# A graph network on one core: 24 instead of 20 of 98 receiver blocks fetched edge by edge, their products placed by time

## The chip, the cores and the metric

The kernel runs on one core of one Trainium2 chip. The metric is device time in microseconds (us) of one execution. The kernel before has a median of 2966.63 us over 10 runs (2956.32 to 2979.18). TensorE multiplies, VectorE (DVE), ScalarE (ACT) and GpSimd (POOL) do the elementwise work, SyncE (SP) issues transfers; POOL also issues the indirect transfers, whose row numbers come from a list on the chip.

## The reference

There are 12500 nodes with 64 features, and 212500 edges sorted by receiver (100000 drawn pairs in both directions and a loop on each node). Cut to what is computed:

```python
def sage(h, Wl, Wr, b):                    # three of these; relu after the first two
    summed = segment_sum(h[src], dst, n)
    cnt = segment_sum(ones(n_edges), dst, n)
    return (summed / maximum(cnt, 1))[...] @ Wl + h @ Wr + b

h = relu(layernorm(x))
x = x + sage(relu(sage(relu(sage(h, ...)), ...)), ...)
h = relu(layernorm(x))
agg = scatter_mean(edge_attr_64, dst)      # of the edges' 64 features
y = relu(concat([agg, h]) @ W0 + b0)
y = relu(y @ W1 + b1) @ W2 + b2
return x + y
```

All is fp32. The kernel splits an fp32 value into three bf16 terms of 64 columns each (192 columns a node), so that sums of them keep the precision.

## The kernel before

**Tiling.** The receivers are 98 blocks of 128 nodes (`NB = 98`). The sum over the neighbours of a block is made in one of two ways. *Fetched* blocks are the first `GB = 20`: a block has at most `EK = 19` times 128 edges; for each 128 edges POOL gathers the senders' rows from DRAM (`got`, 128 x 192 bf16, L461), DVE makes the one-hot matrix of their receivers (`own`, L336, for five products at a time), and TensorE adds their product into `pg` (L489, 128x192). *Dense* blocks are the other 78, in groups of four (`dense_groups`: 19 full groups and one of two blocks): there is a matrix of edge counts from all 12544 senders to the group's 512 receivers, stored as one byte per count and read as fp8. A group takes 98 *whole* products (L392, 128 rows of senders by 512 receivers, the first two bf16 terms, 128 columns of the array) and 98 *half* products (L403, the third term, 64 columns of the array, by turns in its left and right half).

**Stages.** Layer 0 builds the matrices as well: a pair of one-hot tiles (`h` and `c`, DVE, L790 to L792) is multiplied into `pb` (L809, 104 products per group), ACT casts it into the matrix (`m`, L812), and SP stores the matrix (`mat`, L834). Layer 1 reads the matrices back (`t`, L1005). Layer 2 does that too, and also sums the edge features (L1138, 19 products for each of all 98 blocks, with `load` and `cut` ahead of them) and runs the last network on each group (L1167, L1177, L1186).

**The order.** TensorE's order is written out by `Weave`. `run` yields the whole products of a group to position 56 (`TURN`), as many half products, then the remaining 42 of both. Other work is put between them: `wide` work when the count of whole products `w` passes its position, `narrow` work at a given index of a half phase. `spread` puts the use of each fetched product into `wide`, at equal distances (`spot`), so fetched products stand among whole products alone. Their use number i issues the fetch of number i + `NGOT`, as the buffer comes free. `pg` is a tile of two halves, allocated anew for every two blocks, in a pool of one buffer; after each block DVE reduces its half into `ga` (L496), and after every four come transposes (L507), the blocks' own rows turned (L425) and the mixing with the weights (L436 and L440). In layer 0 the matrix fills are spread over 40 `wide` places and, two at a time, over the half-phase indices 6, 20, 34, 48, 62 and 76.

**Index and lists.** In layer 0 `index` finds where each group's edges begin: ACT counts in `heads`, POOL gathers a tile of receivers (`ends`, L567 through `gather`, two buffers), ACT counts in it (L582), and POOL gathers the edges (`to`, `of`). `coded` does that for dense groups, `listed` for four fetched blocks; the latter also has POOL gather the block's 19 x 128 receivers and senders (`l_to`, `l_of`: eight gathers for four blocks), from which DVE makes `place` and `rows_of` (L748 to L756). These steps are hung at fixed distances before the first use of their blocks, or before the start of their group.

Of the kernel before, what the change touches and what calls it, by code (L numbers as in the profile page):

```python
# [11 lines left out]
F32 = mybir.dt.float32  # L12
I32 = mybir.dt.int32
# [6 lines left out]
ALU = mybir.AluOpType  # L20
# [9 lines left out]
P = 128  # L30
D = 64
# [12 lines left out]
WD = 5  # L44
FAR = 1 << 23
EK = 19
GB = 20
H1 = 10
QE = 5

# [21 lines left out]
def in_order(  # L72
# [217 lines left out]
    assert HP % HC == 0  # L290
    RING = HP // HC
    TURN = 2 * HC * (-(-RING // 2))

    class Weave:

        def __init__(self):
            self.w, self.seq, self.wides, self.narrows = 0, 0, [], []

        def wide(self, pos, fn):
            self.seq += 1
            heapq.heappush(self.wides, (pos, self.seq, fn))

        def narrow(self, pos, sub, fn):
            self.seq += 1
# [2 lines left out]
        def run(self, whole, half):  # L309


            half = enumerate(half)
            for n in (TURN, None):
                for _ in islice(whole, n):
                    self.w += 1
                    while self.wides and self.wides[0][0] <= self.w:
                        heapq.heappop(self.wides)[2]()
                for i, _ in islice(half, n):
                    due = [f for f in self.narrows if f[0] <= i and f[1] <= self.w]
                    for f in sorted(due):  # L320
                        self.narrows.remove(f)
                        f[3]()
                    heapq.heapify(self.narrows)

        def rest(self):
            while self.wides or self.narrows:
# [17 lines left out]
    HALVES = ((0, H1), (H1, EK))  # L344
    CUTS = [(k, min(k + QE, EK)) for k in range(0, EK, QE)]
    NC = len(CUTS)
    NGOT = 8

    psd = ctx.enter_context(tc.tile_pool(name="ps_dense", bufs=1, space=PSUM))
    psc = ctx.enter_context(tc.tile_pool(name="ps_conv", bufs=1, space=PSUM))  # L350
    psg = ctx.enter_context(tc.tile_pool(name="ps_got", bufs=1, space=PSUM))
    conv = ctx.enter_context(tc.tile_pool(name="conv", bufs=2))
    gots = ctx.enter_context(tc.tile_pool(name="got", bufs=NGOT))
    owns = ctx.enter_context(tc.tile_pool(name="own", bufs=2))

    class Layer:


        def __init__(self, l, rows, done, gap=0, kept=(conv, 2)):
            self.l, self.rows, self.done, self.gap, self.kept = l, rows, done, gap, kept  # L360
            self.psd, self.psc, self.psg = psd, psc, psg
            self.pool, self.got, self.own = conv, gots, owns
            self.weave = Weave()
            self.turns = 0
            self.fetched, self.owned = {}, {}

# [8 lines left out]
        def hand_over(self, to):  # L375

            w = self.weave
            for pos, _, f in sorted(w.wides, key=lambda a: a[:2]):
# [100 lines left out]
        def use(self, i):  # L479
            b, k = divmod(i, EK)  # L480
            if i == 0:
                self.mark(0, 0)
            if i % (2 * EK) == 0:
                self.pg = self.psg.tile([P, 2, 3 * D], F32, name="pg")
            if i % (4 * EK) == 0:
                self.ga = self.pool.tile([P, 4, D], F32, name="ga", bufs=2)
            if k % QE == 0:
                self.mark(b, k // QE + 1)
            nc.tensor.matmul(  # L489
                self.pg[:, b % 2, :], self.owned.pop(i), self.fetched.pop(i),  # L490
                start=k == 0, stop=k == EK - 1,
            )
            self.fetch(i + NGOT)
            if k + 1 < EK:
                return
            nc.vector.tensor_reduce(  # L496
                self.ga[:, b % 4, :],
                self.pg[:, b % 2, :].rearrange("p (i d) -> p d i", i=3), axis=AX.X, op=ALU.add,
            )
            if b % 4 == 3:  # L500
                ga, j0, w = self.ga, b - 3, self.weave
                box = {}

                def sums():
                    pt = self.psc.tile([D, 4, P], F32, name="pt")
                    for k in range(4):
                        nc.tensor.transpose(pt[:, k, :], ga[:, k, :], ident)  # L507
                    box["agg"] = self.pool.tile([D, 4 * P], F32, name="gat", bufs=1)
                    nc.scalar.copy(box["agg"], pt.rearrange("p k n -> p (k n)"))

                def own_rows():
                    ht = self.turn(j0, 4)
                    w.wide(w.w + 9, lambda: self.mix(box["agg"], ht, j0, 4, inv_u))

                w.narrow(w.w + 1, 40, sums)
                w.narrow(w.w + 1, 68, own_rows)

    steps = NB * len(dense_groups)

    def spot(i, first):  # L520
# [2 lines left out]

    def spread(layer, first):
        for i in range(EK * GB):
            layer.weave.wide(spot(i, first), lambda i=i: layer.use(i))


    TW = 4 * P
# [14 lines left out]
    with ExitStack() as s:  # L544
# [8 lines left out]
            steps = relu_steps(layer.pool, o, t)  # L553
            return steps + [lambda: nc.sync.dma_start(h_d[1][:, j0 : j0 + n, :], t)]

        layer = Layer(0, rows0, done0, gap=6)
        heads = s.enter_context(tc.tile_pool(name="heads", bufs=1)).tile([P, TT], I16, name="heads")
        out0 = s.enter_context(tc.tile_pool(name="out0", bufs=2))
        idx = s.enter_context(tc.tile_pool(name="idx", bufs=1))
# [12 lines left out]
        def index(j, box):  # L572
# [17 lines left out]
            def ends():  # L590

                box["tile"] = tile("tile_of", 1)
                nc.vector.tensor_scalar(
                    box["tile"], box["s"], -0.5, 1.0 - TT / 2, op0=ALU.mult, op1=ALU.max
                )
                tile_i = tile("tile_i", 1, I32)
                nc.vector.tensor_scalar(tile_i, box["tile"], TT / 2 - 1.0, None, op0=ALU.add)
                box["ends"] = tile("ends", TW, I32)
                gather(box["ends"], tiles_d, tile_i[:, :1])

            def inside():
# [321 lines left out]
        with tc.manual_schedule(engines={PE, DVE, ACT, POOL}):  # L923
# [96 lines left out]
    def load(b):  # L1020
        if b is None:
            return

        n = EK * P
        raw = ed.tile([P, n // P * D + 1], F32, name="raw")
        first = raw[:1, n // P * D :].bitcast(I32)
        nc.vector.tensor_scalar(first, mine[:1, b : b + 1], float(EP - n), None, op0=ALU.min)
        at0 = nc.values_load(
            first, engines=[SP], min_val=0, max_val=EP - n,
            skip_runtime_bounds_check_because="it is clamped, and is not under 0",  # L1030
        )
        raw = raw[:, : n // P * D].rearrange("p (k d) -> p k d", d=D)
        nc.sync.dma_start(raw, edge[ds(at0, n), :].rearrange("(p k) d -> p k d", k=EK))
# [4 lines left out]
        nc.sync.dma_start(to, dst[ds(at0, n), :].rearrange("(p k) o -> p (k o)", k=EK))  # L1038
# [739 lines left out]
```

## Time and profile before

| What | Value |
|---|---|
| median of 10 runs | 2966.63 us |
| the profiled execution | 2959.17 us, of which the span is 2957.3 us |
| mean granted TensorE clock | 0.983 |
| layer 0, 1, 2 (from first whole product to the next layer's) | 94 to 1166, 1166 to 1938, 1938 to 2957 us |
| TensorE, whole products (L392) | 5880, 378 ns from start to end, overlapping |
| TensorE, half products (L403) | 5880, 375 to 381 ns, overlapping |
| TensorE, fetched products (L489) | 1140, 247 ns |
| POOL, fetches (L461) | 1140, 1094 ns mean, 1247.4 us in all |
| DMA | 537.43 MB, mean 182 GB/s |
| SP, stores of matrices | 39 of 3136 KB |

The profile is of one execution. Busy time of an engine counts its instructions' spans; matmuls overlap, so what one costs is read from the distance of starts. "Idle before" a group of instructions is the time in which its engine stood, with what ended it. The chain of waits goes back from the last instruction to what released it, step by step. A stretch (window) gives each engine's busy time within it, and the granted clock.

### The profile page before, as it was taken

The page shows a single profiled execution, that of the slowest core. Times are in us where ns is not written, and L with a number is a line of the kernel's source. Part 1 is how long each engine was busy: PE and PEld are TensorE (multiplying, and loading weights), DVE is VectorE, ACT ScalarE, POOL GpSimd, SP SyncE. Part 2 cuts the span into 40 slices and gives each one's busy share as a digit, 9 for nine tenths or more (in the row PEclk, how much of TensorE's full clock was granted, in tenths as well). Part 3 has the DMA queues.
Part 4 walks back from the last instruction along what each step waited for, and adds up shares of the span by engine and source line. Part 5 has one row for each costly group of instructions (what it writes and reads, how often), then busy time and mean ns, then how long its engine had stood idle before and what let it go on. Part 6 is the DMA issues. An engine that isn't in the chain of part 4 may idle for free.

```text
span 2957.3 us, 50078 instructions
## 1 busy us (share of the span) xinstructions
PE 2767.3 (94%) x19505; PEld 1603.0 (54%) x19505; DVE 1630.7 (55%) x3376; ACT 1122.4 (38%) x2339; POOL 1428.5 (48%) x1313
## 2 busy tenths in 40 slices
PE   1699998999999998999999999999999999999997
PEld 0455554555555554555555555565656656565655
DVE  8878777787777772211111111156756656566663
ACT  4666565566666562100000000033333333333332
POOL 5346666566565550455545454434544444445440
PEclk9999999999999999999999999999999999999997
DMA  3434443434434435765645665576767576676661
GB/s 95 173 111 169 159 148 140 161 130 161 164 126 162 164 135 206 230 210 204 208 162 204 207 208 182 182 256 221 223 210 231 175 223 221 213 223 223 209 205 35
DMA packets 203193, 537.43 MB, mean 182 GB/s; under 512 B 83873, under 2 KB 92194, under 8 KB 197954
## 3 DMA queue, kind: packets, MB, share of 16 engines
q1 hardware_dynamic: 143890, 458.08, 42.7%
q0 software_dynamic: 41360, 66.33, 9.7%
q10 hardware_dynamic: 17696, 9.74, 1.1%
q8 instruction: 154, 2.52, 0.4%
q14 instruction: 93, 0.76, 0.1%
HBM read 391.11 MB, written 142.90 MB: 181 GB/s over the span
## 4 chain that ended last, share of the span: by engine, by line
PE 83%; DVE 10%; issue 2%; DMA 1%; ACT 1%; POOL 1%; another core or an unknown queue 0%; SPq 0%; ACTq 0%; DVEq 0%; POOLq 0%
PE p L392 38%; PE p L403 21%; PE pb L809 6%; PE pe L1138 5%; PE pg L489 3%; DVE c L792 3%; PE po L436 3%; PE po L440 3%; PE pt L425 2%; DVE h L790 1%; PE pm L1177 1%; DVE h L791 1%; PE pm L1186 1%; DMA ends<-in_dst_dram,tile_i 1%; PE pm L1167 0%
## 5 line engine op out<-in xcount | busy, mean ns | idle before, releaser
L461 POOL DMA_INDIRECT got<-h_d,rows_of x1140 | 1247.4, 1094 | 1307.6 <-PE pg L489 864.5
L812 ACT CAST m<-pb 128x490 uint16<-128x490 f32 (+1 forms) x1014 | 545.6, 565 | 361.5 <-PE pb L809 281.2
L392 PE MATMUL p<-m,rows 128*128 128x512 fp8e3 (+1 forms) x1960 | 569.0, 378 | 2.7 <-ACT m L812 2.7
L392 PEld LDWEIGHTS <-rows 128*128 128x128 bf16 x3920 | 374.6, 100 | 246.6 <-issue 46.0
L392 PE MATMUL p<-t,rows 128*128 128x512 fp8e3 (+1 forms) x1960 | 490.4, 377 | 0.9 <-ACT rows L263 0.9
L392 PE MATMUL p<-t,m 128*128 128x512 fp8e3 (+1 forms) x1960 | 459.6, 377 | 0.4 <-issue 0.4
L809 PE MATMUL pb<-c,h 128*128 128x245 bf16 x2028 | 374.0, 275 | 84.6 <-ACT m L812 52.2
L336 DVE TENSOR_TENSOR own<-iota_l,place 128x640 bf16<-128x640 bf16 (+3 forms) x280 | 144.1, 515 | 382.0 <-PE pg L489 249.1
L809 PEld LDWEIGHTS <-h 128*128 128x128 bf16 x2028 | 191.0, 99 | 295.6 <-issue 139.0
L403 PEld LDWEIGHTS <-rows 128*64 128x64 bf16 x3920 | 225.3, 110 | 222.2 <-issue 85.1
L489 PE MATMUL pg<-got,own 128*128 128x192 bf16 x1140 | 281.2, 247 | 18.8 <-DVE ga L496 10.9
L792 DVE TENSOR_TENSOR c<-iota_c,col 128x1968 bf16<-128x1968 bf16 (+1 forms) x234 | 298.5, 1275 | 0.0
L392 PEld LDWEIGHTS <-m 128*128 128x128 bf16 x1960 | 184.9, 99 | 189.1 <-issue 26.1
L403 PE MATMUL p<-m,rows 128*64 128x512 fp8e3 (+1 forms) x1960 | 258.0, 381 | 1.9 <-issue 1.6
L403 PE MATMUL p<-t,rows 128*64 128x512 fp8e3 (+1 forms) x1960 | 252.0, 377 | 0.0
L790 DVE TENSOR_TENSOR h<-iota_l,lo 128x1024 bf16<-128x1024 bf16 (+1 forms) x234 | 173.7, 742 | 128.5 <-PE pb L809 84.9
L403 PE MATMUL p<-t,m 128*64 128x512 fp8e3 (+1 forms) x1960 | 233.0, 375 | 7.2 <-issue 5.9
L1052 ACT CAST cut<-raw 128x640 bf16<-128x640 f32 x196 | 136.5, 697 | 242.0 <-PE pe L1138 122.5
L1054 ACT CAST cut<-e_rest 128x640 bf16<-128x640 f32 x196 | 136.8, 698 | 225.5 <-DVE e_rest L1053 190.1
L1055 DVE TENSOR_TENSOR cut<-e_rest,cut 128x640 bf16<-128x640 f32 x196 | 154.9, 790 | 83.8 <-ACT cut L1054 63.0
L1138 PE MATMUL pe<-cut,own 128*128 128x192 bf16 x1862 | 187.7, 248 | 0.0
L1138 PEld LDWEIGHTS <-own 128*128 128x128 bf16 x1862 | 161.1, 99 | 40.2 <-issue 2.2
(189 smaller groups left out, 2564.8 us busy)
## 6 DMA issues: line engine op xcount, KB each, us to landing
t<-mat SPq DMA_DIRECT2D x546, 448.0 KB
mat<-m SPq DMA_DIRECT2D x39, 3136.0 KB
raw<-in_edge_dram SPq DMA_DIRECT2D x98, 608.0 KB
got<-h_d,rows_of POOLq DMA_INDIRECT x1140
h_d<-rows SPq DMA_DIRECT2D x14, 336.0 KB
h_d<-rows ACTq DMA_DIRECT2D x24, 192.0 KB
h_d<-out SPq DMA_DIRECT2D x21, 192.0 KB
m<-h_d SPq DMA_DIRECT2D x6, 576.0 KB
```

Source lines behind the costliest of these rows:

```text
L336: nc.vector.tensor_tensor(t[:, :n].rearrange("p k (c t) -> p k c t", t=2), iota_l.rearrange("p (c t) -> p c t", t=2)[:, None].to_broadcast ...
L392: nc.tensor.matmul(p1, rows[:, i, : 2 * D], at(i), start=i == 0, stop=i == NB - 1)
L403: nc.tensor.matmul(p2[h], rows[:, i, 2 * D :], at(i), start=i < 2, stop=i >= NB - 2)
L461: nc.gpsimd.indirect_dma_start(out=t, out_offset=None, in_=h_rows[self.l], in_offset=bass.IndirectOffsetOnAxis(ap=rows_of[:, b, k : k + 1] ...
L489: nc.tensor.matmul(self.pg[:, b % 2, :], self.owned.pop(i), self.fetched.pop(i), start=k == 0, stop=k == EK - 1,)
L790: nc.vector.tensor_tensor(split(th), pairs(iota_l, P), own(lo, P), op=ALU.is_equal)
L792: nc.vector.tensor_tensor(split(tc_), pairs(iota_c, CW), own(col, CW), op=ALU.is_equal)
L809: nc.tensor.matmul(pb[:, i, : HP * WD], h, c, start=True, stop=True)
L812: nc.scalar.copy(m[:, block // 2, :, o : o + 2 * k].rearrange("p h (w d) -> p h w d", d=k), pb[:, :, : HP * WD].rearrange("p w (h d) -> p ...
L1054: nc.scalar.copy(c[:, :, D : 2 * D], rest)
L1055: nc.vector.tensor_tensor(c[:, :, 2 * D :], rest, c[:, :, D : 2 * D], op=ALU.subtract)
L1138: nc.tensor.matmul(box["pe"], o[:, k - k0, :], c[:, k - k0, :], start=k == 0, stop=k == EK - 1)
```

## The change

`GB` goes from 20 to 24, so one group of four blocks is fetched by edge and no longer dense; 18 full groups and one of two blocks remain. Uses of fetched products go into a new queue, `even`: they are due by slots, of which a whole product is one and a half product is a half, and are taken up after each whole product and, in half phases, at a few indices alone (`stops`): 28 and 77 in layers 1 and 2, the indices of the fills in layer 0. There are ten `got` buffers for eight. The tile of `pg` is allocated once. The lists of the fetched blocks are loaded by SP with plain transfers whose start is read into a register (`first_of`), as the edge features' already were. `ends` has one buffer for two.

```diff
-GB = 20
+GB = 24
...
+    MIDDLES = (TURN // 2, (TURN + NB) // 2)
+    FILLS = tuple(range(6, NB - 14, 14))
...
+        def even(self, pos, fn):
+            self.seq += 1
+            heapq.heappush(self.evens, (pos * 1.5, self.seq, fn))
+
+        def catch_up(self):
+            while self.evens and self.evens[0][0] <= self.slots:
+                heapq.heappop(self.evens)[2]()
...
                 for _ in islice(whole, n):
                     self.w += 1
+                    self.slots += 1
+                    self.catch_up()
...
                 for i, _ in islice(half, n):
+                    self.slots += 0.5
...
+                    if i in self.stops:
+                        self.catch_up()
...
-    NGOT = 8
+    NGOT = 10
...
+    sums_of = psg.tile([P, 2, 3 * D], F32, name="pg")
...
-            if i % (2 * EK) == 0:
-                self.pg = self.psg.tile([P, 2, 3 * D], F32, name="pg")
...
             nc.tensor.matmul(
-                self.pg[:, b % 2, :], self.owned.pop(i), self.fetched.pop(i),
+                sums_of[:, b % 2, :], self.owned.pop(i), self.fetched.pop(i),
...
+    def first_of(at):
+        return nc.values_load(
+            at, engines=[SP], min_val=0, max_val=EP - EK * P,
+            skip_runtime_bounds_check_because="it is clamped, and is not under 0",
+        )
+
+    def in_block(table, at0):
+        return table[ds(at0, EK * P), :].rearrange("(p k) d -> p (k d)", k=EK)
...
-            layer.weave.wide(spot(i, first), lambda i=i: layer.use(i))
+            layer.weave.even(spot(i, first), lambda i=i: layer.use(i))
...
-        layer = Layer(0, rows0, done0, gap=6)
+        layer = Layer(0, rows0, done0, gap=6, stops=FILLS)
...
-                box["ends"] = tile("ends", TW, I32)
+                box["ends"] = tile("ends", TW, I32, 1)
...
+                    box["at"] = idx.tile([1, 4], I32, name="l_at", bufs=2)
+                    nc.vector.tensor_scalar(
+                        box["at"], mine[:1, 4 * j : 4 * j + 4], float(EP - EK * P), None,
+                        op0=ALU.min,
+                    )
                 for k in (k0, k0 + 1):
-                    b = 4 * j + k
-                    gather(box["to"][:, k, :], dst, mine[:, b : b + 1])
-                    gather(box["of"][:, k, :], src, mine[:, b : b + 1])
+                    at0 = first_of(box["at"][:, k : k + 1])
+                    for to, ends in ((box["to"], dst), (box["of"], src)):
+                        nc.sync.dma_start(to[:, k, :], in_block(ends, at0))
...
-                    narrows = [6 + i // 2 * 14 for i in range(len(fills) - nw)]
+                    narrows = [FILLS[i // 2] for i in range(len(fills) - nw)]
```

More of the change, by code (lines that the diff above doesn't have):

```diff
@@ L292, in in_order, with __init__ @@
     TURN = 2 * HC * (-(-RING // 2))
+    MIDDLES = (TURN // 2, (TURN + NB) // 2)
+    FILLS = tuple(range(6, NB - 14, 14))
     class Weave:
-        def __init__(self):
+        def __init__(self, stops):
+            self.stops = stops
             self.w, self.seq, self.wides, self.narrows = 0, 0, [], []
+            self.slots, self.evens = 0, []
         def wide(self, pos, fn):
@@ L323, in run @@
                     heapq.heapify(self.narrows)
+                    if i in self.stops:
+                        self.catch_up()
         def rest(self):
+            assert not self.evens
             while self.wides or self.narrows:
@@ L356, in in_order, with __init__ @@
     class Layer:
-        def __init__(self, l, rows, done, gap=0, kept=(conv, 2)):
+        def __init__(self, l, rows, done, gap=0, kept=(conv, 2), stops=MIDDLES):
             self.l, self.rows, self.done, self.gap, self.kept = l, rows, done, gap, kept
-            self.psd, self.psc, self.psg = psd, psc, psg
+            self.psd, self.psc = psd, psc
             self.pool, self.got, self.own = conv, gots, owns
-            self.weave = Weave()
+            self.weave = Weave(stops)
             self.turns = 0
@@ L377, in hand_over @@
             w = self.weave
+            assert not w.evens
             for pos, _, f in sorted(w.wides, key=lambda a: a[:2]):
@@ L497, in use @@
                 self.ga[:, b % 4, :],
-                self.pg[:, b % 2, :].rearrange("p (i d) -> p d i", i=3), axis=AX.X, op=ALU.add,
+                sums_of[:, b % 2, :].rearrange("p (i d) -> p d i", i=3), axis=AX.X, op=ALU.add,
             )
@@ L1022, in load @@
             return
[L1024 to L1033, printed above, removed]
+        raw = ed.tile([P, EK * D + 1], F32, name="raw")
+        first = raw[:1, EK * D :].bitcast(I32)
+        nc.vector.tensor_scalar(first, mine[:1, b : b + 1], float(EP - EK * P), None, op0=ALU.min)
+        at0 = first_of(first)
+        nc.sync.dma_start(raw[:, : EK * D], in_block(edge, at0))
+        raw = raw[:, : EK * D].rearrange("p (k d) -> p k d", d=D)
         if b < GB:
@@ L1037, in load @@
         to = ed.tile([P, EK], I32, name="e_to")
-        nc.sync.dma_start(to, dst[ds(at0, n), :].rearrange("(p k) o -> p (k o)", k=EK))
+        nc.sync.dma_start(to, in_block(dst, at0))
         at = ed.tile([P, EK, 2], BF16, name="e_at")
```

## The prediction

> **What bounds the kernel now.** I read the busy time first, then the chain of work that ended last.
>
> ```profile
> PE 2767.3 (94%) x19505; PEld 1603.0 (54%) x19505; DVE 1630.7 (55%) x3376; ACT 1122.4 (38%) x2339; POOL 1428.5 (48%) x1313
> ...
> PE p L392 38%; PE p L403 21%; PE pb L809 6%; PE pe L1138 5%; PE pg L489 3%; DVE c L792 3%; PE po L436 3%; PE po L440 3%; PE pt L425 2%; DVE h L790 1%; PE pm L1177 1%; DVE h L791 1%; PE pm L1186 1%; DMA ends<-in_dst_dram,tile_i 1%; PE pm L1167 0%
> ```
>
> TensorE sets the end: it is busy for 94% of the span, and 59% of the chain is the dense products alone, whole (L392) and half-array (L403). By layer it is busy for 911.7 of 959 us (207 to 1166), 746.7 of 772 (to 1938) and 948.7 of 956 (to 2894). So the change is worth the TensorE time it takes out, less what it puts in. For that I cut the trace at the first whole product of a dense group, so that each stretch holds 98 whole and 98 half products, and asked for busy times by stretch (columns: stretch, length, then busy us and count of PE, PEld, DVE, ACT, POOL, then the granted clock, DMA share and GB/s).
>
> ```profile
> 748.63:800.84 52.21, 51.47 (x376) 29.84 (x375) 42.06 (x83) 33.89 (x74) 30.48 (x25) 1.00 0.45 164
> 800.84:860.69 59.85, 55.10 (x377) 31.23 (x376) 44.16 (x94) 36.72 (x90) 33.72 (x29) 1.00 0.41 147
> 860.69:920.39 59.70, 52.44 (x366) 29.66 (x365) 44.43 (x104) 33.16 (x72) 35.92 (x33) 0.97 0.39 138
> 920.39:971.95 51.56, 51.40 (x377) 29.98 (x376) 42.34 (x82) 33.93 (x74) 30.15 (x26) 1.00 0.45 159
> 971.95:1028.04 56.09, 54.69 (x377) 31.92 (x376) 42.27 (x84) 33.81 (x74) 31.68 (x26) 0.97 0.42 150
> ...
> 1329.44:1369.87 40.43, 38.74 (x263) 20.75 (x262) 4.88 (x11) 3.15 (x6) 20.75 (x21) 1.00 0.57 194
> 1369.87:1410.90 41.03, 40.91 (x262) 22.33 (x262) 6.06 (x14) 2.81 (x6) 19.90 (x21) 0.96 0.55 190
> 1410.90:1447.31 36.41, 36.41 (x248) 20.89 (x246) 4.46 (x10) 1.99 (x4) 20.13 (x21) 1.00 0.62 214
> ...
> 2081.91:2129.82 47.91, 47.91 (x357) 28.70 (x356) 31.50 (x61) 18.50 (x32) 24.31 (x20) 1.00 0.72 227
> 2129.82:2179.18 49.36, 49.36 (x375) 30.04 (x373) 31.93 (x64) 19.49 (x34) 23.50 (x21) 1.00 0.69 223
> 2179.18:2233.16 53.98, 53.16 (x381) 31.95 (x379) 34.83 (x73) 20.67 (x37) 22.92 (x20) 1.00 0.65 204
> 2233.16:2282.29 49.13, 49.13 (x366) 29.69 (x365) 31.71 (x61) 18.62 (x32) 22.48 (x21) 1.00 0.69 219
> ```
>
> An undisturbed group takes 51.56 us in layer 0 (which also builds matrices), 36.41 in layer 1, 47.91 in layer 2 (which also sums edge features). The longer stretches are those in which four fetched blocks end: their transposes, rows and mixing are extra work there.
>
> **The change part by part.** *Removed: one dense group of four blocks per layer* (78 dense blocks are 19 groups and a half one, 74 are 18 and a half one). Its stretch goes, except the fetched and edge products in it, which only move to other stretches. A 128x192 product in a row costs 0.082 us: ten L1138 products take 2314.40 to 2315.22 below. Layer 0 gives 51.56 - 23 x 0.082 = 49.7, layer 1 36.41 - 21 x 0.082 = 34.7, layer 2 47.91 - (20 + 95) x 0.082 = 38.5: together -122.9 us. The 104 build products (L809), their casts (L812) and one-hots (L790 to L792) are inside the 49.7.
>
> *Added: 4 x 19 = 76 fetched products per layer*, 3 x 76 x 0.082 = +18.7.
>
> *Added: the ending of four fetched blocks per layer*, from the stretches against an undisturbed one: layer 0 (52.21 - 51.56) + ((59.85 + 56.09)/2 - 51.56) = 7.1; layer 1 4.0 + 4.6 = 8.6; layer 2 1.45 + 6.07 + 1.22 = 8.7: +24.4. These hold small waits and a lower clock. From below, the plain work is L507 (0.5), L425 (0.7) and sixteen L436/L440 (1.8), 9 for three layers; from above, the worse layer-0 stretch makes it 27. I take the observed 24.4.
>
> *Moved: fetched products into half phases.* In layers 1 and 2 they go in at two points of a half phase, 28 and 77. The order of the changed kernel's instructions has 70 new breaks of this kind, all holding L509 alone; in layer 0 they join breaks that the fills already make. No fetched product sits in a half phase before, so the nearest row is layer 0's fills:
>
> ```profile
> 611.72 1.70 PE L403 MATMUL p<-m,rows 128*64 128x512 fp8e3 x14
> 613.35 0.60 PE L809 MATMUL pb<-c,h 128*128 128x245 bf16 x4
> 613.88 1.70 PE L403 MATMUL p<-m,rows 128*64 128x512 fp8e3 x14
> ...
> 1236.84 4.55 PE p L403 x42
> ...
> 2314.40 0.99 PE L1138 MATMUL pe<-cut,own 128*128 128x192 bf16 x10
> 2315.22 0.38 PE L392 MATMUL p<-t,rows 128*128 128x512 fp8e3 x1
> ```
>
> From 611.72 to 613.88 are 14 halves and 4 fills: 2.16 us, where 0.108 per half (42 in 4.55 in the chain) and 0.107 per fill would make 1.94. A break costs 0.21, 70 of them +14.7; bounds 0 (the halves on both sides overlap) and 0.32, that of the first break of a phase (607.38 to 608.89, 7 halves and 4 fills in 1.51 where 1.19 would do), 8 more. A rule of the skill speaks against this part: the Trainium skill, TensorEngine Tiling, Key Properties, says that going from one tiling mode to another drains the array. Its page TensorE: Matmul & The Clock Gate, Single matmul latency, has some 0.175 us for a drain; an estimate with two drains per break is 0.35, 24 in all, 10 us more than by the row. The timeline agrees that a break costs something; its own size is taken.
>
> *Removed: a wait at the bank's turn.* `pg` was allocated anew for every two blocks, so the first product of a pair waited for the reduction of the one just finished. With one tile for good, only the reduction two blocks back matters, 19 products away.
>
> ```profile
> PE pg L489 <- DVE ga L496: 10.9, 9, 1.8
> ```
>
> I take -10.9; bounds 0 (if the halves of the bank still wait on each other) and -16, since after the wait at 2325.6 the clock was 0.93, 0.90 and 0.66 in three stretches of 10 us, 5 us more.
>
> *Moved: lists from POOL to SP.* Per four blocks 8 gathers leave POOL (8 x 1.4 us of its queue) and SP gets 4 register loads and 8 transfers. Behind a waiting SP stand the stores of `mat` and `h_d`; a `mat` buffer is needed again a whole group later (50 us), which covers them. The lists are used 30 or more whole products after issue, some 16 us; if they are late, DVE waits at L748 and the one-hots behind it after two batches. Cost nothing. There is one list more (five become six) for one built matrix less. Stretches with two indices took 51.85 (639.27 to 691.12) and 59.70: 0.3 to 8.1 over an undisturbed one; I take +3. On the other side, TensorE stood for 6.29 us at 496.5 and 3.64 at 894 while POOL issued a list among long runs of gathers; if the gathers cause that, -10. I can't show that they do, so 0.
>
> *Changed: one `ends` buffer for two.* In the changed order two of its gathers stand next to each other on POOL once, and overlap partly at one more place. The second waits for ACT's pass over the first, and fetches queue behind it. Ten `got` buffers at one use per 1.8 us (1552 wholes, 15.8 groups of some 53 us, for 456 uses) cover about 18 us, about the wait. But then ACT's two passes follow each other and the second waits for a landing. Landings on the chain took 3.62, 5.68 and 12.20 us: +4, bounds 0 and 18.
>
> Sum: -122.9 + 18.7 + 24.4 + 14.7 - 10.9 + 3 + 4 = **-69 us**. The profiled execution took 2959.2 (span 2957.3 and 1.9 around it), 7.4 under the median of 2966.6; on the median this is 2966.6 - 69 = **2897 us**.
>
> **The rivals.** *POOL becomes the bound (slower).* It must issue 456 fetches per layer instead of 380. Mean of one fetch by layer:
>
> ```profile
> L461 POOL DMA_INDIRECT got<-h_d,rows_of x372 | 443.6, 1192 | 328.1 <-PE pg L489 197.5 <-PE pb L809 62.7 <-issue 54.0
> ...
> L461 POOL DMA_INDIRECT got<-h_d,rows_of x380 | 365.9, 963 | 424.1 <-PE pg L489 240.0 <-DMA h_d<-m 79.0 <-issue 62.5
> ...
> L461 POOL DMA_INDIRECT got<-h_d,rows_of x380 | 428.6, 1128 | 544.1 <-PE pg L489 427.0 <-issue 62.7 <-PE pe L1138 51.2
> ```
>
> With the 0.30 us between two, one fetch takes 1.49, 1.26 and 1.43. In layer 1 the uses lie between wholes 90 and 1772 of 1862, 90% of about 755 us (772 less this layer's part of the sum): 1.49 us per use, so POOL is 85% taken; in layer 0 it is 456 x 1.49 + 60 gathers x 1.5 = 770 of about 920, 84%. Against this rival: POOL mostly waits for TensorE (`PE pg` above), and even spacing takes away the crowding at 4.34 wholes (about 1.0 us) per use. It decides above 1.49 us per fetch in layer 1, and outweighs the gain only above (680 + 69)/456 = 1.64, 30% over the row. At 1.70 there: 456 x 0.21 = 96 lost, 2966.6 - 69 + 96 = 2994. Chance 0.06.
>
> *Breaks are dearer.* If each stop also waits for weights, landings or the one-hots of a burst of two or three products and costs 0.75, 70 x 0.54 = 38 more: 2935. For it: only 0.21 was seen with fills, whose operands lay ready. Chance 0.17.
>
> *The stalls were POOL's and the bank's.* Long list runs gone (-10), the lower clock after the bank waits too (-5), endings nearer their plain work (-15): 2867. For it: the lower clocks (0.96, 0.97) stand in just those stretches; against it: the mixes that lower it remain. Chance 0.20.
>
> *The gain is given back* in layer 0 by the `ends` wait and starving fetches at every index (25 x 2.8 us): 2967, no change. Chance 0.03.
>
> **How the numbers follow.** The forecast has 0.54. The unknowns from their good ends (list -10, endings -15, bank -5, breaks -8) make 2859; from their bad ends, not all at once (breaks +8, `ends` +14, bank +11, list +5), 2935. The range 2859 to 2936 takes in the two faster rivals. A measurement here tells about 0.3% (9 us) from no change. Faster: 0.54 + 0.17 + 0.20 = 0.91; same 0.03; slower 0.06.
>
> **What would show it.** Right: L392's and L403's successors at 5586 each with unchanged means; 19 groups a layer; no wait of `pg` for `ga`; undisturbed groups of about 53, 37.5 and 49 us, each with 26 to 29 fetched products. Wrong: `pg` waiting for `got` landings, POOL over 90% taken in a stretch, TensorE idle over 5 us at the two joined `ends` gathers, halves around a stop more than 0.3 us apart, or DVE waiting at L748's successor. The forecast falls if fetches slow down when they no longer pause.

## The result, and the profile after

The changed kernel took 3019.13 us (median of 9 runs, 3008.13 to 3029.15) where the kernel before took 2967.84 (31 runs): the ratio is 1.0172, 95% interval 1.0152 to 1.0193. The forecast was 2897. The profiled execution of the changed kernel has a span of 3014.9 us at a mean granted clock of 0.967, against 2957.3 at 0.983.

The counts are as forecast: 19 groups a layer, 5586 whole and half products, 1368 fetched ones. The page of the changed kernel, busy time and the row of the fetches:

```profile
PE 2754.5 (91%) x19052; PEld 1580.5 (52%) x19052; DVE 1615.8 (54%) x3398; ACT 1090.2 (36%) x2287; POOL 1591.8 (53%) x1501
...
L483 POOL DMA_INDIRECT got<-h_d,rows_of x1368 | 1457.8, 1066 | 1166.0 <-PE pg L509 654.3
```

TensorE has less to do and stands for longer: 91% where it had 94%. No other engine is near full. POOL still idles for 654 us until a fetched product of TensorE frees a buffer, so it is no bound. Stretches of single groups, cut as in the prediction (length, then busy us and count of PE, PEld, DVE, ACT, POOL, then clock, DMA share and GB/s):

```profile
839.68:921.05 81.37, 64.53 (x389) 36.66 (x389) 47.23 (x109) 36.73 (x88) 42.29 (x38) 0.85 0.32 108
1094.19:1144.30 50.11, 50.05 (x358) 29.02 (x358) 29.80 (x41) 30.07 (x56) 27.12 (x23) 1.00 0.43 156
1620.02:1672.71 52.69, 45.70 (x268) 24.27 (x267) 7.50 (x17) 2.81 (x6) 26.87 (x29) 0.88 0.52 174
1672.71:1710.39 37.68, 37.68 (x252) 19.50 (x251) 4.95 (x11) 1.98 (x4) 23.11 (x24) 0.99 0.57 184
2632.67:2683.42 50.75, 50.45 (x380) 29.92 (x378) 32.36 (x65) 19.32 (x34) 27.95 (x27) 1.00 0.66 217
```

The second, fourth and fifth are undisturbed groups, near the 53, 37.5 and 49 that the prediction named. The others are not: a layer-1 group of 52.69 has 7 us in which TensorE stands, and a clock of 0.88. Over the trace after 210 us, TensorE's gaps above 0.3 us come to 151.7 us (81.4 before), and the lower clock costs 98.5 us of full-speed time (47.5 before, both summed from the clock's records; a little of it lies within the gaps). The two differences, 70 and 51, make 121. The span grew by 57.6, so all the rest is some 64 shorter, near the 69 of the forecast: gaps and clock are where it went wrong.

One such gap, instruction by instruction (start, length, engine and line, count, and the idle time before it with its releaser):

```profile
1436.94 2.56 PE L425 MATMUL p<-t,m 128*64 128x512 fp8e3 x22
1437.35 0.94 POOL L483 DMA_INDIRECT got<-h_d,rows_of  x1 [0.30 <-issue]
...
1439.44 0.26 PE L509 MATMUL pg<-got,own 128*128 128x192 bf16 x1
1439.85 0.94 POOL L483 DMA_INDIRECT got<-h_d,rows_of  x1 [0.30 <-issue]
1442.96 0.80 SPq L1040 DMA_DIRECT2D t<-mat  x2
1443.10 0.36 DVE L516 TENSOR_REDUCE ga<-pg 128x64 f32<-128x192 f32 x1 [9.47 <-remote]
1443.33 0.94 POOL L483 DMA_INDIRECT got<-h_d,rows_of  x1 [2.54 <-remote]
1443.51 0.24 PE L509 MATMUL pg<-got,own 128*128 128x192 bf16 x1 [3.81 <-DVE ga L516]
```

The last product of a block ends at 1439.70. DVE has nothing to do, yet its reduction starts at 1443.10; SP's load of `t` and POOL's next fetch start within the same 0.4 us. TensorE waits 3.81 for the reduction, which itself takes 0.36. But for POOL's fetch of 0.94 and the end of a copy on ACT nobody was busy in between. I read this as news that came late: TensorE was done, and all who waited for it learned it some 3 us later. POOL had been issuing fetches one after another since 1428.5. The kernel before has such gaps too, the 6.29 at 496.5 and the 3.64 at 894 that the prediction names.

To count this, I took every instruction of DVE and ACT that reads one of six kinds of TensorE's results (`ga`, `m`, `e`, `ht`, `e_sum`, `gat`; over 1100 in a trace), and called it a *late user* if it starts over 1 us after both the product before it has ended and its own engine is free. The kernel before has 36, the changed one 33. The time at which TensorE's own completion signals are recorded was not used for this, because in the traces of the changed kernel that have late users only 3528 to 3588 of 4265 such records are present.

### The profile page after: what moved, and what is told of

Read it like the earlier page. It is cut to its first block, busy times and chain, and to the rows that moved or that the text cites. A ratio compares the mean times of both kernels' runs of the same rounds, so it can differ in the third digit from the quotient of the medians.

```text
span 3014.9 us, 49685 instructions
## 1 busy us (share of the span) xinstructions
PE 2754.5 (91%) x19052; PEld 1580.5 (52%) x19052; DVE 1615.8 (54%) x3398; ACT 1090.2 (36%) x2287; POOL 1591.8 (53%) x1501
## 3 DMA queue, kind: packets, MB, share of 16 engines
q0 software_dynamic: 47376, 77.16, 10.4%
## 5 line engine op out<-in xcount | busy, mean ns | idle before, releaser
L483 POOL DMA_INDIRECT got<-h_d,rows_of x1368 | 1457.8, 1066 | 1166.0 <-PE pg L509 654.3
L847 ACT CAST m<-pb 128x490 uint16<-128x490 f32 (+1 forms) x962 | 515.1, 565 | 388.3 <-PE pb L844 309.5
L414 PE MATMUL p<-m,rows 128*128 128x512 fp8e3 (+1 forms) x1862 | 552.9, 384 | 0.8 <-ACT m L847 0.8
L414 PE MATMUL p<-t,rows 128*128 128x512 fp8e3 (+1 forms) x1862 | 467.8, 376 | 0.0
L356 DVE TENSOR_TENSOR own<-iota_l,place 128x640 bf16<-128x640 bf16 (+2 forms) x336 | 173.0, 516 | 462.8 <-PE pg L509 275.9
L509 PE MATMUL pg<-got,own 128*128 128x192 bf16 x1368 | 306.1, 249 | 31.1 <-DVE ga L516 22.2
L425 PEld LDWEIGHTS <-rows 128*64 128x64 bf16 x3724 | 208.9, 110 | 216.5 <-issue 93.9
L827 DVE TENSOR_TENSOR c<-iota_c,col 128x1968 bf16<-128x1968 bf16 (+1 forms) x222 | 283.2, 1276 | 0.0
L425 PE MATMUL p<-t,rows 128*64 128x512 fp8e3 (+1 forms) x1862 | 233.1, 376 | 1.2 <-issue 1.2
L509 PEld LDWEIGHTS <-own 128*128 128x128 bf16 x1368 | 129.1, 99 | 138.0 <-issue 41.8
```

The source lines that it names most:

```text
L356: nc.vector.tensor_tensor(t[:, :n].rearrange("p k (c t) -> p k c t", t=2), iota_l.rearrange("p (c t) -> p c t", t=2)[:, None].to_broadcast ...
L414: nc.tensor.matmul(p1, rows[:, i, : 2 * D], at(i), start=i == 0, stop=i == NB - 1)
L425: nc.tensor.matmul(p2[h], rows[:, i, 2 * D :], at(i), start=i < 2, stop=i >= NB - 2)
L483: nc.gpsimd.indirect_dma_start(out=t, out_offset=None, in_=h_rows[self.l], in_offset=bass.IndirectOffsetOnAxis(ap=rows_of[:, b, k : k + 1] ...
L509: nc.tensor.matmul(sums_of[:, b % 2, :], self.owned.pop(i), self.fetched.pop(i), start=k == 0, stop=k == EK - 1,)
L827: nc.vector.tensor_tensor(split(tc_), pairs(iota_c, CW), own(col, CW), op=ALU.is_equal)
```

## The experiments

Ratios are to the kernel before on the same chip in the same session, with 95% intervals; five rounds each.

Sessions came in two kinds. In two of them the kernel before took 2896.0 and 2892.9, and no trace of any kernel has a late user. In the others, the first pair included, it took 2947 to 2972 and all kernels but one have some. Below, "in time" and "late" mean these two. Chip number 15 gave one session of each kind, so it is not the chip alone; what sets it I could not find out. One candidate was not tested, the recording of the executions: each of them has a recorded span and clock, and late traces lack many records of signals where the changed kernel's trace in time has 4261 of 4265. Whether the lateness would be there without a recording is not shown.

### First session, in time: which part costs?

The theories were: A, POOL's long runs of gathers make TensorE's signals late; B, fetched products now stand in bursts of two or three, and a burst that crosses a block's border waits for the reduction. Four edits:

```diff
# 24 blocks alone, on the kernel before
-GB = 20
+GB = 24
# the even placement alone (and one allocation of `pg`, ten buffers): the changed kernel with
-GB = 24
+GB = 20
-tile("ends", TW, I32, 1)
+tile("ends", TW, I32)
# ... and the lists on POOL as before
# no even placement, on the changed kernel
-layer.weave.even(spot(i, first), ...)
+layer.weave.wide(spot(i, first), ...)
# half the gathers, on the changed kernel, in fetch(); half the rows are not the edges'
+            if i % 2:
+                self.fetched[i] = self.fetched[i - 1]
+                return
```

> The kernel before with 24 fetched blocks for 20 and nothing else of the change: fetched products are still spaced by whole products, eight buffers, two `ends` buffers, lists on POOL (l_hi is written over l_of to save 304 bytes). Theory A (POOL's longer unbroken runs of gathers make TensorE's completion signals late, and whoever waits for them is late): 456 gathers a layer are crowded into the whole phases, so much of the loss is here already: 2960 to 3010. Theory B (bursts of two or three fetched products as neighbours, above all over a block's border, where the next product waits for the reduction of the block just ended): there are no bursts here, so the terms of the forecast without breaks hold, 2966.6 - 122.9 + 18.7 + 24.4 + 3 = 2890, at most 2910.

> The changed kernel with 20 fetched blocks for 24, lists back on POOL and two `ends` buffers: what is left of the change is the even placement with its stops, and ten buffers for eight. Theory A: POOL issues as many gathers as before, but pauses less, 2975 to 3000. Theory B: the bursts are as dense as their rate, five sixths of those of the changed kernel; if they cost the 122 us that the forecast missed, this takes 2967 + 100 = 3065, and at least 3030.

> The changed kernel with its fetched products spaced by whole products again, as before; 24 blocks, ten buffers, one `ends` buffer and lists on SP stay. Theory A: the number of gathers stays, most of the loss stays: 2975 to 3020. Theory B: bursts and breaks gone, 2966.6 - 122.9 + 18.7 + 24.4 + 3 + 4 = 2894, at most 2915.

> The changed kernel in which every second fetched product takes the rows of the one before it, so that half of the gathers (228 a layer) are left out; TensorE's instructions and their order stay. Theory A: POOL's runs are short, signals come in time: 2900 or less. Theory B: bursts, borders and breaks are all still there: 3000 or more.

Measured: 24 blocks alone 0.9860 (0.9832 to 0.9888; 2852.04 against 2896.01); the even placement alone 1.0160 (1.0129 to 1.0190); the change without it 0.9787 (0.9760 to 0.9815); half the gathers 0.9888 (0.9863 to 0.9914). It looked like B, though half the gathers was far below B's 3000. But the traces have no late user at all, so these four runs could say nothing on A. The changed kernel itself had not been run beside them, and came next.

### Second and third session, late: controls and single parts

```diff
# lists on POOL: the changed kernel with the gathers of the kernel before in edges()
# borders apart, in catch_up(); use() returns whether it ended a block
-                heapq.heappop(self.evens)[2]()
+                if heapq.heappop(self.evens)[2]():
+                    break
# no stops in the half phases of layers 1 and 2
-    MIDDLES = (TURN // 2, (TURN + NB) // 2)
+    MIDDLES = ()
```

> The changed kernel itself, once more, as a control: in the four runs before this the kernel before took 2896 where it had taken 2968, and their traces show no completion signal of TensorE over 1 us late, where the two first traces have hundreds. If the late signals belong to the place where the first two were run, the changed kernel is here near the kernel with half its gathers, 0.985 to 0.995 of the kernel before (theory A holds, but only for that place). If they belong to the changed kernel, 1.017 as measured first.

> The changed kernel with its lists fetched by gathers on POOL again, as before; all else as changed. The forecast had the move at 0, or 10 gained by it: 0 to 10 more than the control. If the register loads and waits on SP cost something, it is less than the control by more than 5.

> The changed kernel in which a burst of fetched products ends with a block: the first product of the next block waits for the next place. Theory B (the border within a burst): 20 to 50 less than the control where signals come late, 8 to 19 less where they come in time (19 to 21 waits of pg for ga, 15 to 19 us in the traces of these runs). If the wait costs nothing that is not lost anyway: within 5 of the control.

> The changed kernel without the two stops in the half phases of layers 1 and 2: what would have been made up there goes in one burst at the start of the next whole phase. The forecast has 70 breaks at 0.21 there: 15 less than the control, if longer bursts cost nothing; 38 more than that if each break costs 0.75. If longer bursts starve for fetched rows or for one-hots: more than the control.

> The changed kernel as a control for the kernel beside it, and to see whether the traces with late signals and those without belong to the chip. Where signals come late (the kernel before at 2950 to 2970): 1.010 to 1.020 of the kernel before, as in the control before this. Where they come in time (the kernel before at about 2896): the kernel with half its gathers took 0.989 there, the even placement alone 1.016; both the theory of late signals and the burst theory then give 0.985 to 1.005.

> The changed kernel with its fetched products spaced by whole products again, a second time. Where signals come in time it took 0.979: 0.975 to 0.983 again. Where they come late: if the even placement is what makes their lateness cost time (bursts that wait for the round trip of a border, and gathers that follow each other without a pause), 0.975 to 0.985 as well; if the number of gathers alone makes the lateness, 1.000 to 1.015.

Measured: the changed kernel 1.0135 (1.0104 to 1.0166) and 1.0137 (1.0110 to 1.0164); lists on POOL 1.0296 (1.0268 to 1.0325); borders apart 1.0114 (1.0074 to 1.0154); no stops 1.0431 (1.0402 to 1.0460); without the even placement **1.0455** (1.0423 to 1.0487), where the same file had 0.9787 in the first session.

So B falls as the cause of the loss in late sessions: with the borders apart the ratio's interval overlaps the control's, and taking the even placement away makes the kernel 3.1% slower than the control (3081.22 for 2989.17), not faster. The file without it shows what lateness does. A stretch of it in layer 1, in each session (columns as above):

```profile
1166.39:1203.14 36.75, 36.75 (x252) 19.84 (x250) 5.37 (x12) 1.99 (x4) 24.86 (x26) 1.00 0.64 213
```

```profile
1431.53:1485.85 54.32, 46.53 (x253) 23.75 (x252) 5.72 (x13) 1.98 (x4) 26.49 (x28) 0.85 0.45 148
```

The same 252 or 253 products take 36.75 in time and 54.32 late. In the late session the half products themselves stop, although they wait for nothing that the profile shows (timeline of the same kernel; bracket: idle time before):

```profile
1504.13 0.94 POOL L483 DMA_INDIRECT got<-h_d,rows_of  x1 [0.30 <-issue]
1504.33 0.38 PE L425 MATMUL p<-t,m 128*64 128x512 fp8e3 x1 [0.29 <-issue]
...
1505.38 0.94 POOL L483 DMA_INDIRECT got<-h_d,rows_of  x1 [0.30 <-PE p L425]
1505.72 0.42 PE L425 MATMUL p<-t,m 128*64 128x512 fp8e3 x2 [1.01 <-issue]
...
1507.15 0.59 PE L425 MATMUL p<-t,m 128*64 128x512 fp8e3 x1 [1.01 <-issue]
```

Pauses above 0.2 us between two half products number 78 here, and there are none in the first session. Some 30 of them lie within an unbroken run of eight or more gathers on POOL, and 45 more in the 5 us after one. So it is not late signals alone: TensorE's own issue stops as well.

### Fourth session, late: is it the gathers?

```diff
# half the gathers: as in the first session
# 20 blocks, all else as changed
-GB = 24
+GB = 20
# rows by SP, in fetch(); the rows are not the edges'
-            nc.gpsimd.indirect_dma_start(out=t, ..., in_=h_rows[self.l], ...)
+            nc.sync.dma_start(t, h_d[self.l][:, i % GB, :])
# lists on SP alone: the kernel before with the changed lists only (and one allocation of `pg`)
```

> The changed kernel with every second fetched product taking the rows of the one before it: 228 gathers a layer for 456, TensorE's instructions unchanged. Where signals come late (the kernel before near 2950): if the gathers delay the signals, the lateness over 1 us falls to less than a third of the changed kernel's and the time to 0.985 to 0.995 of the kernel before, the ratio measured where signals come in time; if the lateness belongs to TensorE's own bursts and breaks, 1.010 to 1.020.

> The changed kernel with 20 fetched blocks for 24: even placement, ten buffers, one `ends` buffer and lists on SP stay. Where signals come late: the lists on SP gained 1.6% and the even placement 3.2% at 24 blocks, so if it is the gathers of the four more blocks that cost the time, this beats the kernel before: 0.975 to 0.990. If the placement costs by itself, as it did where signals come in time (1.016): 1.000 to 1.015.

> The changed kernel in which each fetched tile is loaded by one plain transfer from SP's queue (128 rows of the same 384 bytes, of block i modulo 24) for a gather by POOL: the fetched rows are not those of the edges. The same bytes land, POOL makes no descriptors for them. If POOL's making of gathers is what delays TensorE's signals: hardly a signal over 1 us late in layers 1 and 2, and 0.960 to 0.990 of the kernel before. If the transfers themselves do it: lateness as in the changed kernel, 1.010 or more.

> The kernel before (20 blocks, spaced by whole products, eight buffers, two `ends` buffers) with its lists on SP and nothing else of the change. Where signals come late: at 24 blocks with even placement the move was worth 1.6%, most of it in layer 0; 0.985 to 0.995 here, as there are five lists for six and eight gathers less in each of POOL's crowded stretches. If the move is worth nothing at this spacing: 0.997 to 1.003.

Measured: half the gathers 0.9730 (0.9702 to 0.9757), 7 late users; 20 blocks 0.9955 (0.9940 to 0.9971), 6; rows by SP 0.9616 (0.9595 to 0.9637), none; lists on SP alone 0.9875 (0.9852 to 0.9898), 31. The page of the kernel with rows by SP, and a layer-1 stretch of it:

```profile
PE 2692.7 (94%) x19052; PEld 1560.8 (55%) x19052; DVE 1611.5 (56%) x3398; ACT 1094.9 (38%) x2287; POOL 132.7 (5%) x133
```

```profile
1165.00:1202.00 37.00, 37.00 (x250) 19.22 (x248) 4.95 (x11) 1.98 (x4) 0.00 (x0) 1.00 0.67 211
```

TensorE runs the changed kernel's products in the changed kernel's order, the same number of bytes lands at the same places, and POOL's fetches are gone: the lateness with them, in a session where the lists on SP alone have 31 late users. (The changed kernel itself was not run in the fourth session.) Layer 1 takes 740.2 us here, 739.6 in the changed kernel in time (fifth session) and 809.6 in its first trace: without POOL's fetches the late session costs this layer nothing. So A holds, as far as it says that in late sessions the lateness comes with POOL's gathers. It is not the amount that is moved (211 GB/s here, 174 in the 52.69 group above). Which part of a gather does it is not shown: the run takes away POOL's instructions, the queue that they use and the scattered rows at once.

### Fifth and sixth session: what was left

```diff
# two `ends` buffers, on the changed kernel (and NGOT = 9 for 10, two list tiles in place, for room)
-tile("ends", TW, I32, 1)
+tile("ends", TW, I32)
# six stops: the same, and
-    MIDDLES = (TURN // 2, (TURN + NB) // 2)
+    MIDDLES = FILLS
```

> The changed kernel with two `ends` buffers as before (nine fetched-row buffers for ten, and two helper tiles of the lists written in place, to make room). The forecast had the single buffer at 4, bounds 0 and 18. If it is the single buffer that makes the thirteenth group of layer 0 75 to 81 long with 13 to 17 of idle time in the changed kernel: that group falls to 60 or less and the kernel to 12 to 20 under the control. If the long group is POOL's gathers in a row, however many buffers: within 5 of the control.

> The kernel before with its lists on SP alone, a second time, on whichever chip: 0.985 to 0.990 of the kernel before where signals come late, as measured. Where they come in time the gathers that it takes off POOL delay nobody: 0.990 to 1.000.

> The changed kernel as the control for the two beside it: 1.010 to 1.020 of the kernel before where signals come late; where they come in time, 0.985 to 1.000 (half the gathers 0.989, no even placement 0.979).

> The changed kernel with two `ends` buffers (as in the run before this, nine fetched-row buffers) and with layer 0's six stops in the half phases of layers 1 and 2 for two. Layer 1's clean groups of the control and of the kernel without even placement, 37.42 and 36.75 for the same 26 products, price a break at (37.42 - 36.75)/2 = 0.34; four more in each of 36 groups cost up to 36 x 4 x 0.34 = 49 where signals come in time: 0.987 + 0.017 = 1.004 of the kernel before. Where they come late, no stop instead of two cost 3%, so if it is the evenness of the gathers that keeps signals in time, the gain outweighs the breaks: below 1.006 (the changed kernel's 1.0135 less the 0.7% of the buffer); if not, 1.020 or more.

The fifth was in time: two `ends` buffers 0.9869 (0.9842 to 0.9895; 2858.72), lists on SP alone 0.9972 (0.9957 to 0.9987), and the changed kernel itself **0.9942** (0.9923 to 0.9961; 2877.22 against 2892.85). The sixth was late: six stops with two `ends` buffers 0.9960 (0.9936 to 0.9983), 15 late users.

So the change gains 0.6% where signals come in time and loses 1.4 to 1.7% where they come late, both under 2%. Together, for the late sessions (POOL's operations after 210 us, and the share of them that stand in unbroken runs of eight or more):

| Kernel | ratio | POOL operations | in runs of 8+ | late users |
|---|---|---|---|---|
| rows by SP | 0.9616 | 56 | 0 | 0 |
| half the gathers | 0.9730 | 736 | 0.24 | 7 |
| lists on SP alone | 0.9875 | 1186 | 0.44 | 31 |
| 20 blocks | 0.9955 | 1187 | 0.14 | 6 |
| six stops, two `ends` | 0.9960 | 1416 | 0.36 | 15 |
| before (first pair) | 1 | 1219 | 0.45 | 36 |
| borders apart | 1.0114 | 1416 | 0.48 | 35 |
| changed (control of the second session) | 1.0135 | 1415 | 0.45 | 33 |
| lists on POOL | 1.0296 | 1455 | 0.49 | 53 |
| no stops | 1.0431 | 1415 | 0.59 | 47 |
| no even placement | 1.0455 | 1414 | 0.63 | 64 |

At 24 blocks the late users rise by and large with the share in long runs, and the time with them (lists on POOL and borders apart are out of order). Long runs alone do not do it: in time the share of the changed kernel is 0.66, and no user is late. Six stops for two bring fewer late users again, and with two `ends` buffers 0.9960, where the control's 1.0135 less the 0.7% of the buffer would be 1.006: more evenness gained more than its breaks cost, as far as two sessions can be compared. 20 blocks in an even placement have few late users, but pay for the placement and for the products of the dense group that stays.

Half the gathers and rows by SP do not sum the right rows. Of the versions that compute the reference, the lists on SP alone beat the kernel before in both kinds of session (0.9875 and, by little, 0.9972), and the changed kernel where signals come late. In time the changed kernel with two `ends` buffers is better (0.9869), and the one without the even placement best (0.9787), though that one is the worst of all when late.

## Why the prediction was wrong

**The step that failed** is a sentence of the part on the lists: TensorE stood for 6.29 us at 496.5 and 3.64 at 894 "while POOL issued a list among long runs of gathers; if the gathers cause that, -10. I can't show that they do, so 0." The stalls had been seen, but were charged to the lists, which leave POOL, and priced at nothing. In late sessions such stalls come with POOL's gathers of any kind, and the change adds 76 gathers a layer. In its own terms, the forecast gave 228 more fetched products 0.082 us each on TensorE, and their gathers nothing as long as POOL has time for them. From the in-time control to the first pair, the kernel before loses 2967.84 - 2892.85 = 75 us to lateness and the changed one 3019.13 - 2877.22 = 142: lateness costs the change 67 us of the 120 between the forecast of -69 and the measured +51. (These are different sessions, and for the first pair the chip is not on record; in the second session, where the loss was 35, the same sum gives 51.)

**The other 53** show in time, where the forecast of -69 met -16:

| Term | forecast | measured in time |
|---|---|---|
| groups out, products and endings in, one list more | -76.8 | -72 (worked out: -62 without the even placement, less the two rows below) |
| even placement, with the wait for the bank | 14.7 - 10.9 = +3.8 | +45 (0.9942 against 0.9787 of 2893; 38 between the two profiled executions) |
| single `ends` buffer | +4 | +18 (2877.22 against 2858.72) |
| lists to SP | 0 | -8 (2892.85 against 2884.69) |

The sum is -17. *Dense groups, products, endings*: right, within 5 us, if the other rows add up as taken; -72 is what they leave, and no run has this part by itself. With the lists on POOL and eight buffers 24 blocks gain 40 us only (by the ratio; 44 by the medians); TensorE then waits 26.5 us, 25 times, for rows to land, which ten buffers and the lists on SP bring to 3.9.

*The wait for the bank* did not go. "With one tile for good, only the reduction two blocks back matters" is wrong. Two waits, of the changed kernel, and of the one without the even placement (us, times, longest):

```profile
PE pg L509 <- DVE ga L516: 22.2, 18, 3.8
```

```profile
PE pg L509 <- DVE ga L516: 19.3, 20, 3.2
```

It was 10.9, 9 times; in time the changed kernel has 22.7, 21 times, so lateness is not the reason. In the timeline at 1443.51 above the first product of a block follows the reduction of the block just ended; in the traces of both kernels this holds at odd borders as at even ones, though the two halves of `pg` are different. In the kernel before, 4 of the 9 waits stand in the middle of a pair, where nothing is allocated: the allocation was never the cause. This term's sign was wrong, +11 for -10.9, and its bound of 0 was too.

*Breaks*: layers 1 and 2 each take 13.3 us more with the even placement than without it (739.6 for 726.3, 970.8 for 957.5; control of the fifth session against the first), 26.6 where 14.7 was forecast. The skill's drain (the Trainium skill, TensorE: Matmul & The Clock Gate, Single matmul latency) gave an estimate of 24 to 25 there, nearer than the row of the fills. The timelines show why. Half products of layer 1 without a break, and with one (without the even placement, then the fifth session's control):

```profile
1198.49 4.72 PE L425 MATMUL p<-t,m 128*64 128x512 fp8e3 x42
```

```profile
1209.73 2.56 PE L425 MATMUL p<-t,m 128*64 128x512 fp8e3 x22
1212.23 0.34 PE L509 MATMUL pg<-got,own 128*128 128x192 bf16 x2
1212.50 2.35 PE L425 MATMUL p<-t,m 128*64 128x512 fp8e3 x20
```

From the first half product to the next whole one this is 4.66 and, less 0.082 for each fetched product, 4.88: 0.22 for the break. In the first half phase of a group it is 6.86 and 7.27, so 0.41. Both repeat from group to group of layer 1. On the average a break costs 0.32, the upper bound of the prediction, and at that price 70 make 22 of the 26.6. The row of the fills was too cheap. What the rest is was not tried; layer 0 adds 12, 7 of them in one group.

*`ends`*: the group with the two joined gathers is the longest in the trace. Layer 0's group 13 of the in-time control, and of the kernel with two buffers:

```profile
800.33:875.01 74.68, 63.99 (x390) 35.96 (x389) 47.33 (x109) 36.83 (x88) 43.98 (x38) 0.86 0.33 118
```

```profile
798.19:862.42 64.23, 59.67 (x389) 34.95 (x389) 47.07 (x109) 36.95 (x88) 37.96 (x34) 0.92 0.37 132
```

The mechanism was right: the second gather waits for ACT's pass over the first, and fetches queue behind it. In the control POOL stands for 25.14 us until that pass is through (the name that the view gives is that of another engine):

```profile
816.24 0.71 ACT L612 ACTIVATE signs<-ends,before 128x512 int8<-128x512 int32 x1
...
817.31 2.01 POOL L597 DMA_INDIRECT ends<-in_dst_dram,tile_i  x1 [25.14 <-DVE h L826]
```

The ten buffers were to cover some 18 of it. The bound of 18 was right and the value taken was too small. Of the 18, 10 are in this group; it was expected to fall to 60 or less and fell to 64.23.

*Lists to SP*: little in time, 0.3% or 8 us where the forecast has 0, but -1.25% alone in a late session and -1.6% on the changed kernel: the -10 that I could not show, and more.

**The rivals.** None was it by itself. *Breaks are dearer* had the right direction, at 0.75 each where 0.32 was measured. POOL does not become the bound: its fetch in layer 1 takes 0.96 us in the first pair and 0.97 in the in-time control, and TensorE waits 1.9 us in all for rows to land. The nearest was the one that gave the stalls to POOL and the bank, with the sign reversed: the change does not take these stalls away, it brings more of them.

## What to carry to other kernels

A queue that has time left can still cost: an engine that builds transfers in software may slow the handshakes of the others while it does, and this shows as idle time with no busy engine in it. When a profile has a stall in which nobody works, look at what the quiet engine was doing and price the change by that, before calling it unexplained and zero. And run the control in the same session as each experiment: the same file was 2.1% faster and 4.6% slower than the same kernel before.

## What the runs showed of the hardware

- In late sessions users of TensorE's results start late: DVE, SP and POOL 3.3 to 3.6 us after the product in the timeline shown, and ACT is among the late users that were counted. POOL is mostly in or just behind a long run of indirect transfers then: of the 33 late users of the second session's control, 27 are due in a run of eight or more gathers or in the 5 us after one, which together fill 41% of the span. In time, the same gathers, as long (0.97 us), delay nobody.
- The Trainium skill, DMA: Bandwidth & Descriptors, SWDGE vs HWDGE vs iDMA, says that POOL's transfers have their descriptors computed in software, SP's in hardware. The runs agree: the queue that the profile calls software_dynamic has 47376 packets in the changed kernel and 3600 with rows by SP. No user is late with 1368 loads from SP, 33 are with as many gathers (in another late session). That the computing of descriptors is what makes them late no run here shows.
- The Trainium skill, Perfetto Trace Analysis, Per-engine timelines, says that the way of a signal to the other engines lies outside the reported slice. Here the time between the product's end, as the profile has it, and the reduction's start on a free DVE grew from 0.04 us at most in time to 3.4 in the first trace of the changed kernel.
- A gap is paid twice. The granted clock is 1.00 up to and in the gap at 1439.70 of the changed kernel, 0.63 in the 4.5 us after it, and 0.99 in the next 5. The whole stretches of 81.37, 52.69 and 54.32, which hold such gaps, have 0.85 to 0.88, undisturbed ones 1.00 or 0.99.

```profile
1439.70:1443.50 3.80, 0.00 (x0) 0.00 (x0) 0.40 (x2) 0.28 (x1) 1.11 (x2) 1.00 0.12 26
1443.50:1448.00 4.50, 4.49 (x25) 1.84 (x25) 0.98 (x2) 0.00 (x0) 1.72 (x2) 0.63 0.88 300
```
